# Attention and a depthwise convolution on one core: the convolution's products on TensorE regrouped, and ScalarE's long work moved within a unit

## The chip, the cores and the metric

The kernel runs on one core of one Trainium2 chip. A core has five engines with an instruction stream each: TensorE (PE in the profile; its weight loads are PEld), VectorE (DVE), ScalarE (ACT), GpSimd (POOL) and SyncE (SP, which here only issues DMAs). They run side by side and wait for each other through semaphores. Matrix products are written to PSUM, everything else lies in SBUF. The metric is the device time of one execution in microseconds, as the median of a few runs; lower is better.

## The reference

The input x has 16 images of 384 channels of 32 x 32, in f32. Two layers follow each other, each with a residual and a group norm without weights:

```python
# layer 0: attention over the 1024 positions, 8 heads of 48
x = x + _L0_conv_ref(_gn(x), w_qkv, w_proj, b_proj)
# layer 1: depthwise convolution, 7 x 7, padding 3
x = x + _L1_conv_ref(_gn(x), weight)
# where _L1_conv_ref first symmetrises the weight:
w_sym = (weight + rot90(weight, 1) + rot90(weight, 2) + rot90(weight, 3)) * 0.25
# and _gn(v) normalises over 32 groups of 12 channels of one image
```

The depthwise convolution has one 7 x 7 kernel per channel and adds nothing over channels.

## The kernel before

One image after the other (b = 0 to 15), three tiles of 128 channels each (k = 0, 1, 2). For each image TensorE makes q and k (qk_step, L446), v (v_step, L472) and then 64 steps of attention: s_step (L517) makes the scores of a step, ScalarE takes their exponential (L525), av_step (L537) multiplies with v. Sixteen steps are a unit, four units an image. Scores run four steps ahead of av_step, and seven at a unit's start. The scores lie in one of three PSUM buffers (pool ps_s), the sums of a unit in two (ps_o). When a unit is done, take copies its sums out on ScalarE (L550) and the next unit's av_step may use them. The projection of image b (L598) is made while image b + 1 starts; its residual and its statistics lead to the group norm of layer 1.

The convolution of image b is done during the attention of image b + 1, by VectorE, tile by tile: ScalarE writes the normalised tile with padding (fold_x, "padded", L692) and three scaled copies of it (fold_first, "rows_e", L703, three instructions), and VectorE folds the taps (fold_ops, L721 to L734). A tile takes VectorE some 40 us.

The order of all instructions is written by the program itself, under a manual schedule: each engine runs its own list strictly as it was emitted. A small planner keeps two clocks, clock for TensorE and vclock for VectorE, and emits VectorE's work up to a given time (catch_up, which takes due work from the list later, and otherwise the next piece of the fold, tap). Long work for ScalarE (the applications of a norm, rows_e, squares) waits in the list applies with a due time and a planned cost; act_slot takes from it what is due and not dearer than a limit. Between the steps of the attention between_steps calls it with the limit 4.3 us.

In the last image there is no attention of a next image to hide the convolution. Three tiles are therefore convolved on TensorE (PE_TILES: tile 2 of image 14, tiles 2 and 1 of image 15); VectorE does tile 0 of image 15 at the same time. The normalised tile goes to DRAM (conv_store, L875) and comes back in shifted copies (conv_load, L882): partition (q, c) of a shifted tile holds channel c of 32 from row q on, for q = 0 to 3. A product (conv_on_pe, L913) has 32 channels times 4 rows as its 128 terms and 32 channels of one row out; seven columns and two groups of four rows are 14 taps, for each half of the picture, with four products in one tap, one for every 32 channels. The matrices are the kernel's weights on diagonals (conv_matrices, L863). A finished tile is copied out by ScalarE and added to the residual by an accumulating DMA on GpSimd's queue (conv_on_pe_end, L926 and L927), the last one by VectorE from PSUM, a half at a time (conv_on_pe_half, L934), and stored.

The tail is laid out by hand. fast_finish ends the projection of image 15, fast_end makes its statistics with small products (groups_on_pe, L334) and starts the norm (x1_chains: conv_begin, conv_store). Pieces of the convolution of (14, 2), called conv_piece, are put in between, so that TensorE has work while VectorE makes means and variances. Then a loop runs the rest of the pieces; loads emits the next shifted copies.

Of the kernel before, what the change touches and what calls it, by code (L numbers as in the profile page):

```python
# [16 lines left out]
P = 128  # L17
# [28 lines left out]
def kernel(  # L46
# [73 lines left out]
    def run(general):  # L120
        tag = "g" if general else "f"
        with ExitStack() as stack:
# [79 lines left out]
            eye = wpool.tile([P, P // 4], F32, name="eye")  # L202
# [10 lines left out]
            wsh = wpool.tile([P, 2, 4, 2, KS], F32, name="wsh")  # L213
# [445 lines left out]

            def conv_begin(st, b, k, engine):  # L660
                name = f"xn1_{b}_{k}"
                if general:
                    xn1s[b, k] = npool.tile([P, N], F32, tag="xn1", name=name)
                elif b == B - 1:
                    xn1s[b, k] = flat(epool.tile([P, 2, HALF], F32, tag="e", name=name))
                else:
                    xn1s[b, k] = tpool.tile([P, N], F32, tag="t", name=name)
                st.apply(xn1s[b, k], x1s[b, k], k, engine)
# [149 lines left out]
            SH, CH = 4, P // 4  # L818
            ROWS = H // 2 + 4
            XROWS = H + 2 * PAD + 1  # L820
            XW = XROWS * W

            def conv_prepare():

                w_d = dconv.tile([C, 2 * SH * KS], F32, tag="w", name="w_d")
                zero = tpool.tile([P, N], F32, tag="t", name="zero")[:, 0 : SH * W]
                nc.gpsimd.memset(zero, 0.0)
                w_rows = w_d.rearrange("(k p) t -> p k t", p=P)
                with nc.allow_non_contiguous_dma(reason="small, once"):
                    nc.gpsimd.dma_start(  # L830
                        w_rows[:, :, 0 : KS * KS], wsym.rearrange("p k i j -> p k (i j)")
                    )
                    nc.gpsimd.dma_start(
                        w_rows[:, :, KS * KS :],
                        zero[:, 0 : NK * KS].rearrange("p (k t) -> p k t", k=NK),
                    )
                    for n, k in enumerate(PE_K):
                        for q in range(2 * SH):
                            nc.gpsimd.dma_start(
                                wsh[CH * (q % SH) : CH * (q % SH + 1), n, :, q // SH, :],  # L840
                                bass.AP(
                                    w_d.tensor,
                                    w_d.offset + (k * P * 2 * SH + q) * KS,
                                    [[2 * SH * KS, CH], [CH * 2 * SH * KS, SH], [1, KS]],
                                ),
                            )
                for bk in PE_TILES:
                    xds[bk] = dconv.tile([P, XW], F32, tag=f"x_{len(xds)}", name=f"xd_{len(xds)}")
                    nc.gpsimd.dma_start(xds[bk][:, 0 : PAD * W], zero[:, 0 : PAD * W])
                    nc.gpsimd.dma_start(xds[bk][:, (PAD + H) * W :], zero)  # L850
                for q in range(SH):
                    src = ident[:, CH * q : CH * (q + 1)]
                    if q == 0:
                        nc.gpsimd.tensor_copy(eye, src)
                    else:
                        nc.gpsimd.tensor_tensor(eye, eye, src, ALU.add)

            def conv_matrices(n, dst):

                nonlocal vclock  # L860
                dst = dst[:, 0 : SH * 2 * KS * CH].rearrange("p (i t c) -> p i t c", i=SH, c=CH)
                for i in range(SH):
                    nc.vector.tensor_tensor(  # L863
                        dst[:, i],
                        eye.unsqueeze(1).to_broadcast([P, 2 * KS, CH]),
                        wsh[:, n, i].rearrange("p b d -> p (b d)").unsqueeze(2).to_broadcast(
                            [P, 2 * KS, CH]
                        ),
                        ALU.mult,
                    )  # L870
                mats[PE_K[n]] = dst
                vclock += 2.2

            def conv_store(b, k):
                nc.sync.dma_start(xds[b, k][:, PAD * W : (PAD + H) * W], xn1s[b, k])  # L875

            def conv_load(b, k, h, a):

                t = qkpool.tile([P, 2, N], F32, tag="qk", name=f"sh_{b}_{k}_{h}_{a}")
                xd = xds[b, k]  # L880
                for q in range(SH):
                    (nc.scalar if late.get("tail") and q % 2 else nc.sync).dma_start(  # L882
                        t[CH * q : CH * (q + 1), :, 0 : ROWS * W],
                        bass.AP(
                            xd.tensor,
                            xd.offset + 2 * a * CH * XW + (h * H // 2 + q) * W,
                            [[XW, CH], [CH * XW, 2], [1, ROWS * W]],
                        ),
                    )
                shs[b, k, h, a] = t  # L890


            PE_TAPS = [(d0, dx) for d0 in range(2) for dx in range(-PAD, PAD + 1)]
            PE_TAPS.sort(key=lambda t: t[1] != 0)

            def conv_on_pe(b, k, h, first, last):
                if (b, k) == PE_TILES[-1]:

                    if (b, k, h) not in pss:
                        pss[b, k, h] = ps_o.tile([P, HALF], F32, tag="acc", name=f"ps_conv_{h}")  # L900
                    dst = pss[b, k, h]
                else:
                    if (b, k) not in pss:
                        pss[b, k] = psum(f"ps_conv_{b}_{k}")
                    dst = pss[b, k][:, h, :]
                taps = PE_TAPS
                for n, (d0, dx) in enumerate(taps):
                    if not first <= n < last:
                        continue
                    _, (ox, ix) = region(0, dx)  # L910
                    for i in range(SH):
                        src = shs[b, k, h, i // 2][:, i % 2, 0 : ROWS * W]
                        nc.tensor.matmul(  # L913
                            dst[CH * i : CH * (i + 1), :].rearrange("p (y x) -> p y x", x=W)[:, :, ox],
                            lhsT=mats[k][:, i, d0 * KS + dx + PAD, :],
                            rhs=src.rearrange("p (y x) -> p y x", x=W)[
                                :, SH * d0 : SH * d0 + H // 2, ix
                            ],
                            start=(n == 0),
                            stop=(n == len(taps) - 1),  # L920
                        )

            def conv_on_pe_end(b, k):

                t = tpool.tile([P, N], F32, tag="t", name=f"conv_{b}_{k}")
                nc.scalar.copy(t, flat(pss.pop((b, k))))  # L926
                nc.gpsimd.dma_start(x1s[b, k], t, accum_op=ALU.add)  # L927
                conv_end(b, k)

            def conv_on_pe_half(b, k, h):  # L930

                c = slice(h * HALF, (h + 1) * HALF)
                dst = x1s[b, k][:, c]
                nc.vector.tensor_tensor(dst, pss.pop((b, k, h)), dst, ALU.add)  # L934
                (nc.scalar, nc.sync)[h].dma_start(
                    out[b, k * P : (k + 1) * P].rearrange("p h w -> p (h w)")[:, c], dst
# [164 lines left out]
            def catch_up(to):  # L1101
# [20 lines left out]
                (bk, h, a)  # L1122
                for bk in PE_TILES
                for h in range(2)
# [78 lines left out]
            def between_steps():  # L1203
                catch_up(clock)
                if clock >= act_free:
                    act_slot(4.3, 2.3)

            def x1_chains(b, st):
                nonlocal vclock
                on_pe = [t for t in PE_TILES if t[0] == b]  # L1210
                for k in range(NK - 1, -1, -1):
                    if (b, k) in on_pe:
# [3 lines left out]
                        cuts = (0, 4, 8, 10, 12) if b == B - 2 else (0, KS)  # L1216
                        cuts = (*cuts, len(PE_TAPS))
                        pe_conv.extend((b, k, 0, *c) for c in zip(cuts, cuts[1:]))
                        pe_conv.extend(((b, k, 1, 0, KS), (b, k, 1, KS, cuts[-1])))
# [119 lines left out]
            def loads(n):  # L1339
                while n and pe_loads and pe_loads[0][0] in xn1s:  # L1340
                    (b, k), h, a = pe_loads.popleft()
                    conv_load(b, k, h, a)
                    n -= 1

            def conv_piece():
                nonlocal clock
                b, k, h, first, last = pe_conv.popleft()
                while (b, k, h, 1) not in shs and pe_loads:
                    loads(1)
                conv_on_pe(b, k, h, first, last)  # L1350
                clock += 6.2 * (last - first) / KS
                if last == len(PE_TAPS):
                    loads(2)
                    if (b, k) == PE_TILES[-1]:
                        after(2.0, 0.7, lambda: conv_on_pe_half(b, k, h))
                    elif h == 1:
                        after(6.0, 1.2, lambda: conv_on_pe_end(b, k))
# [52 lines left out]
            def fast_end(b):  # L1410
                assert not applies
                x1_stats[b].groups_on_pe(late["masks"], tap, conv_piece)
                conv_piece()
                x1_chains(b, x1_stats[b])

# [6 lines left out]
            for b, n0, size in [  # L1422
# [9 lines left out]
                if ending:  # L1432
# [4 lines left out]
                    loads(2)  # L1437
                for n in range(n0, n0 + size):
# [3 lines left out]
                    between_steps()  # L1442
# [12 lines left out]
                if b == B - 1:  # L1455

                    if once("mat_0", r >= 16):
                        mat = flat2(xpool.tile([P, NK, N], F32, tag="x", name="mat_0"))
                        conv_matrices(0, mat)
                        late["w3"] = mat[:, 2 * SH * KS * CH :][:, 0:C]  # L1460
# [22 lines left out]
            clock += 7.0  # L1483
            vclock = clock
            after(4.0, 1.2, check_vector)
            while later or state["done"] < len(order) or active or pe_conv:
                if pe_conv:
                    if pe_conv[0][0] == B - 1 and lims:
                        check_tensor(lims.pop())
                    conv_piece()  # L1490
                else:
# [54 lines left out]
```

## Time and profile before

| | us |
|---|---|
| median of 3 runs | 2886.64 (2883.92 to 2887.82) |
| the profiled execution | 2884.99 |
| its span, first to last instruction | 2883.1 |
| granted TensorE clock, mean | 0.998 |
| qk products, busy | 502.5 |
| score and av products, busy | 1088.2 each |
| exponentials on ScalarE, busy | 1024.3 |
| products of the convolution on TensorE, first to last | 2798.99 to 2876.7 |

In a timeline a line gives start, length, engine, source line, operation, output and inputs with their shape, and how many instructions of one kind were put together; in square brackets stands the time that the engine was idle before, and what ended it. A matrix product in f32 leaves two records, and records of neighbouring products overlap, so that the pace is read from one start to the next and not from the length of a record. "ACTq" and "SPq" are DMA issues, which don't count as busy. A line of the list of waits gives who waited for whom, the time in total, how often, and the longest.

### The profile page before, as it was taken

How to read it: one execution, taken by the hardware profiler on the slowest of the kernel's cores; microseconds unless marked ns; L12 is line 12 of the kernel's file. 1: busy time of each engine (PE TensorE's matmuls, PEld its weight loads, DVE VectorE, ACT ScalarE, POOL GpSimd, SP SyncE). 2: the span in 40 equal slices, each digit the busy share in tenths (PEclk: the TensorE clock that was granted, in tenths of full speed). 3: DMA queues.
4: the chain of work that ended last, by engine and by line, in shares of the span. 5: the costliest groups of instructions: out<-in, count | busy, mean ns of one | idle time of the engine just before them, and what ended most of it. 6: DMA issues, size and time to landing. Idle time of an engine off the chain costs nothing.

```text
span 2883.1 us, 46610 instructions
## 1 busy us (share of the span) xinstructions
PE 2860.5 (99%) x19654; PEld 1345.2 (47%) x19654; DVE 2080.2 (72%) x2247; ACT 1650.4 (57%) x1921; POOL 244.9 (8%) x398
## 2 busy tenths in 40 slices
PE   9999999999999999999999999999999999999999
PEld 5343445445454444545445454454544445454333
DVE  4504949858597695968959597695968958598776
ACT  3637647475664746647375573746647475574731
POOL 3201012010101001010010101001010010100000
PEclk9999999999999999999999999999999999999999
DMA  6521121211212112130211212112130211212225
GB/s 241 185 39 47 42 65 31 50 49 44 63 33 59 46 36 64 34 73 24 50 49 44 63 31 55 52 29 65 32 80 24 47 53 42 65 31 43 71 71 134
DMA packets 75467, 169.98 MB, mean 59 GB/s; under 512 B 31872, under 2 KB 33808, under 8 KB 73712
## 3 DMA queue, kind: packets, MB, share of 16 engines
q0 software_dynamic: 32320, 108.03, 14.4%
q1 hardware_dynamic: 41216, 55.21, 7.3%
q10 hardware_dynamic: 1712, 3.67, 0.5%
q8 instruction: 156, 2.56, 0.4%
q14 instruction: 63, 0.52, 0.1%
HBM read 118.61 MB, written 28.72 MB: 51 GB/s over the span
## 4 chain that ended last, share of the span: by engine, by line
PE 92%; ACT 4%; DVE 2%; issue 1%; DMA 0%; SPq 0%; ACTq 0%; DVEq 0%
PE ps_s L517 28%; PE acc L537 27%; PE ps_qk L446 17%; PE ps_v L472 9%; PE ps_proj L598 8%; ACT rows_e L703 2%; PE ps_conv L913 2%; ACT e L525 2%; PE ps_proj_last L642 1%; DVE x L734 1%; DVE side L721 0%; PE warm L1280 0%; DVE rows_o L727 0%; PE ps_st_x L334 0%; DMA sum<-o 0%
## 5 line engine op out<-in xcount | busy, mean ns | idle before, releaser
L525 ACT ACTIVATE e<-ps_s 128x1024 f32<-128x1024 f32 x1024 | 1024.3, 1029 | 452.2 <-PE ps_s L517 451.7
L517 PE MATMUL ps_s<-qk 48*64 48x512 f32 x8192 | 1088.2, 589 | 13.4 <-ACT e L525 13.4
L537 PE MATMUL acc<-e,v 64*64 64x512 f32 x8192 | 1088.2, 589 | 1.3 <-ACT e L525 0.5
L537 PEld LDWEIGHTS acc<-e,v 64*64 64x64 f32 x8192 | 426.1, 132 | 461.6 <-issue 444.7
L517 PEld LDWEIGHTS ps_s<-qk 48*64 48x64 f32 x8192 | 410.1, 132 | 490.2 <-issue 433.5
L721 DVE TENSOR_TENSOR side<-padded 128x1024 f32<-128x1024 f32 x270 | 328.3, 1216 | 355.6 <-ACT padded L692 355.6
L724 DVE SCALAR_TENSOR_TENSOR rows_e<-side,even,rows_e 128x1024 f32<-128x1024 f32 x405 | 508.3, 1273 | 9.9 <-ACT rows_e L703 8.4
L446 PE MATMUL ps_qk<-x,wqk 128*128 128x512 f32 x1152 | 502.5, 595 | 0.0
L446 PEld LDWEIGHTS ps_qk<-x,wqk 128*128 128x128 f32 x1152 | 218.2, 190 | 277.8 <-issue 270.8
L734 DVE TENSOR_TENSOR x<-x,rows_o 128x992 f32<-128x992 f32 (+3 forms) x271 | 310.7, 1147 | 3.0
L734 DVE TENSOR_TENSOR x<-x,rows_e 128x992 f32<-128x992 f32 (+2 forms) x270 | 310.8, 1151 | 0.0
L453 ACT COPY qk<-ps_qk 128x1024 f32<-128x1024 f32 x96 | 97.2, 1012 | 365.0 <-PE ps_qk L446 365.0
L472 PE MATMUL ps_v<-wv,x 128*128 128x384 f32 x768 | 252.6, 486 | 0.0
L598 PE MATMUL ps_proj<-o,wp 128*128 128x512 f32 x540 | 234.2, 592 | 0.0
L472 PEld LDWEIGHTS ps_v<-wv,x 128*128 128x128 f32 x768 | 145.9, 190 | 108.2 <-issue 14.3
L492 ACT COPY v<-ps_v 64x384 f32<-64x384 f32 x256 | 121.6, 475 | 120.6 <-PE ps_v L472 118.0
L724 DVE SCALAR_TENSOR_TENSOR rows_o<-side,odd,rows_o 128x1024 f32<-128x1024 f32 x135 | 172.8, 1280 | 1.6
L724 DVE SCALAR_TENSOR_TENSOR x<-side,even,x 128x1024 f32<-128x1024 f32 x135 | 172.5, 1278 | 0.0
L598 PEld LDWEIGHTS ps_proj<-o,wp 128*128 128x128 f32 x540 | 102.6, 190 | 126.2 <-issue 118.1
L811 POOL DMA_DIRECT2D out<-x x45 | 25.3, 563 | 1510.3 <-DVE x L734 1392.9
L703 ACT ACTIVATE rows_e<-padded,even 128x1024 f32<-128x1024 f32 x135 | 147.0, 1166 | 0.0
L606 ACT ACTIVATE x<-ps_proj,bp 128x1024 f32<-128x1024 f32 x45 | 50.1, 1114 | 167.5 <-PE ps_proj L598 167.5
(142 smaller groups left out, 1030.3 us busy)
## 6 DMA issues: line engine op xcount, KB each, us to landing
x<-in_x POOLq DMA_DIRECT2D x90, 512.0 KB, 5.5
inv<-inv SPq DMA_DIRECT2D x126, 256.0 KB
out<-x POOLq DMA_DIRECT2D x45, 512.0 KB, 3.0
xs<-in_x POOLq DMA_DIRECT2D x42, 512.0 KB, 6.2
qk<-qk POOLq DMA_DIRECT2D x96, 128.0 KB, 4.1
o<-o SPq DMA_DIRECT2D x180, 32.0 KB
sh<-xd SPq DMA_DIRECT2D x32, 160.0 KB
x<-in_x SPq DMA_DIRECT2D x6, 512.0 KB
```

What stands on the lines that cost most here:

```text
L446: nc.tensor.matmul(ps[:, h, :], lhsT=wqk[:, k, s, t, :], rhs=xns[b][:, k, h * HALF : (h + 1) * HALF], start=(k == 0), stop=(k == NK - 1),)
L453: nc.scalar.copy(halves(qks[u][:, s, :]), ps)
L472: nc.tensor.matmul(ps[:, j, 0:C], lhsT=xns[b][:, k, t * P : (t + 1) * P], rhs=wv[:, k, :], start=(k == 0), stop=(k == NK - 1),)
L492: nc.scalar.copy(dst[:, :, 0 : HEADS // 2 * (D + 1)].rearrange("p k (h d) -> p k h d", d=D + 1)[:, :, :, 0:D], src.rearrange("p k (h d) -> ...
L517: nc.tensor.matmul(ps[64 * c : 64 * c + 64, a, :], lhsT=qk[r, 1, 64 * kb : 64 * kb + 64], rhs=qk[r, 0, h * HALF : (h + 1) * HALF], start=True,
L525: nc.scalar.activation(es[n], ps, AF.Exp, scale=SCALE)
L537: nc.tensor.matmul(accs[a][64 * j : 64 * j + 64, :], lhsT=v[rows, kb, c : c + 64], rhs=e[rows, j, :], start=(kb == 0), stop=(kb == 2 * NT ...
L598: nc.tensor.matmul(ps[:, h, :], lhsT=wp[:, t, o * P : (o + 1) * P], rhs=os_[b, t // 2][:, t % 2, h * HALF : (h + 1) * HALF], start=(t == 0 ...
L703: nc.scalar.activation(grid(rows_e[dy - 1]), padded_view(i), AF.Identity, scale=even[:, k, dy, 0:1],)
L721: vec.tensor_tensor(grid(sides[n]), padded_view(i, j), padded_view(i, -j), op)
L724: vec.scalar_tensor_tensor(dst, src, w, dst, ALU.mult, ALU.add)
L734: vec.tensor_tensor(dst, dst, src[:, lo + dy * W : hi + dy * W], op)
```

## The change

One product now has 16 channels times 8 rows as its terms and 16 channels of two neighbouring rows as its 32 outputs. A half is no longer the upper or lower half of the picture but half of the channels (a = 0, 1), of all 16 pairs of rows; seven taps of four products make it complete. The normalised tile is written to DRAM with even and odd rows apart (by_rows, PLANE), so that a shifted copy is again one piece of 2 KB a channel; a load is eight copies of 16 partitions instead of four of 32 partitions.

The outputs now come in the order (16 channels, row of the pair, 16 channels, ...). They are therefore copied to SBUF (conv_take), put in order by two products with a permutation matrix for each half (conv_perm) and added by VectorE from PSUM (conv_add); the accumulating DMAs go. In between_steps the limit for ScalarE's work is 1.4 instead of 4.3 in the last five steps of a unit. In the tail fast_end itself emits padded, then two loads, then rows_e, then the takes and the permutation of (14, 2). The pieces of (14, 2) are cut anew, and the two loads in first_half are gone.

```diff
             def between_steps(r):
                 catch_up(clock)
                 if clock >= act_free:
-                    act_slot(4.3, 2.3)
+                    act_slot(1.4 if r % (2 * NT) >= 11 else 4.3, 2.3)
...
+            RI, CG = KS + 1, P // (KS + 1)
+            NG = P // CG
+            PLANE = (H // 2 + PAD) * W
...
+            def conv_load(b, k, a):
+
+                t = qkpool.tile([P, 2, N], F32, tag="qk", name=f"sh_{b}_{k}_{a}")
+                t = t.rearrange("p a n -> p (a n)").rearrange("p (g n) -> p g n", n=HALF)
                 xd = xds[b, k]
+                for i in range(RI):
+                    (nc.scalar if late.get("tail") and i % 2 else nc.sync).dma_start(
+                        t[CG * i : CG * (i + 1)],
...
+            PE_TAPS = sorted(range(-PAD, PAD + 1), key=lambda dx: dx != 0)
...
+                for n in range(first, last):
+                    dx = PE_TAPS[n]
                     _, (ox, ix) = region(0, dx)
+                    for i in range(NG // 2):
+                        src = shs[b, k, a][:, i]
                         nc.tensor.matmul(
+                            dst[2 * CG * i : 2 * CG * (i + 1), :].rearrange("p (y x) -> p y x", x=W)[
+                                :, :, ox
                             ],
+                            lhsT=mats[k][:, NG // 2 * a + i, dx + PAD].rearrange("p t c -> p (t c)"),
+                            rhs=src.rearrange("p (y x) -> p y x", x=W)[:, :, ix],
                             start=(n == 0),
+                            stop=(n == KS - 1),
+                        )
...
+            def conv_take(b, k, a):
+                if a == 0 or (b, k) not in shs:
+                    shs[b, k] = epool.tile([P, 2, HALF], F32, tag="e", name=f"rows_{b}_{k}")
+                nc.scalar.copy(shs[b, k][:, a, :], pss.pop((b, k, a)))
+
+            def conv_perm(b, k, a):
+
+                nonlocal clock
+                if (b, k) not in pss:
+                    pss[b, k] = psum(f"ps_rows_{b}_{k}")
+                part = slice(64 * a, 64 * a + 64)
+                for row in range(2):
+                    nc.tensor.matmul(
+                        pss[b, k][part, row, :],
+                        lhsT=perm[:, row],
+                        rhs=shs[b, k][:, a, :],
+                        start=True,
+                        stop=True,
+                    )
+                clock += 2.2
+                if (b, k) == PE_TILES[-1]:
+                    after(0.5, 1.3, lambda: conv_add(b, k, part, (nc.scalar, nc.sync)[a]))
+                elif a == 1:
+                    after(3.5 if b < B - 1 else 0.5, 1.3, lambda: conv_add(b, k, slice(0, P), nc.gpsimd))
+
+            def conv_add(b, k, part, queue):
+                dst = by_rows(x1s[b, k][part])
+                nc.vector.tensor_tensor(dst, grids(pss[b, k][part]), dst, ALU.add)
+                queue.dma_start(
...
-                        cuts = (0, 4, 8, 10, 12) if b == B - 2 else (0, KS)
-                        cuts = (*cuts, len(PE_TAPS))
-                        pe_conv.extend((b, k, 0, *c) for c in zip(cuts, cuts[1:]))
-                        pe_conv.extend(((b, k, 1, 0, KS), (b, k, 1, KS, cuts[-1])))
+                        cuts = ((0, 4, KS), (0, 2, KS)) if b == B - 2 else ((0, KS), (0, 2, KS))
+                        for a in range(2):
+                            pe_conv.extend((b, k, a, *c) for c in zip(cuts[a], cuts[a][1:]))
...
             def fast_end(b):
+                nonlocal clock, vclock
                 assert not applies
-                x1_stats[b].groups_on_pe(late["masks"], tap, conv_piece)
-                conv_piece()
+                x1_stats[b].groups_on_pe(late["masks"], tap, lambda: conv_piece(False))
+                conv_piece(False)
                 x1_chains(b, x1_stats[b])
+                clock = now()
+                vclock = clock + 1.0
+                after(0.0, 1.2, check_vector)
+                heapq.heappop(applies)[-1]()
+                loads(2)
+                clock += 3.0
+                heapq.heappop(applies)[-1]()
+                conv_rows()
+                clock += 4.5
...
                     first_half(b)
-                    loads(2)
```

## The prediction

> **What bounds the kernel now.** First the page's busy times, then TensorE's list of waits:
>
> ```profile
> PE 2860.5 (99%) x19654; PEld 1345.2 (47%) x19654; DVE 2080.2 (72%) x2247; ACT 1650.4 (57%) x1921; POOL 244.9 (8%) x398
> ...
> PE ps_s L517 <- ACT e L525: 13.4, 14, 1.0
> ```
>
> TensorE is the bound nearly everywhere, so a microsecond is won where TensorE waits or where it has less to do at the end. One wait repeats 14 times. The timelines of TensorE and ScalarE at one of the 14, and at a unit's end without it:
>
> ```profile
> 442.07 1.90 PE L517 MATMUL ps_s<-qk 48*64 48x512 f32 x16
> 444.93 1.09 PE L517 MATMUL ps_s<-qk 48*64 48x512 f32 x8 [0.96 <-ACT e L525]
> 445.84 2.85 PE L537 MATMUL acc<-e,v 64*64 64x512 f32 x24
> ...
> 498.30 2.85 PE L517 MATMUL ps_s<-qk 48*64 48x512 f32 x24
> 500.88 2.85 PE L537 MATMUL acc<-e,v 64*64 64x512 f32 x24
> ...
> 440.72 3.25 ACT L703 ACTIVATE rows_e<-padded,even 128x1024 f32<-128x1024 f32 x3
> 443.86 1.02 ACT L525 ACTIVATE e<-ps_s 128x1024 f32<-128x1024 f32 x1
> 444.77 1.08 ACT L550 COPY o<-acc 128x512 f32<-128x512 f32 x2
> ```
>
> The three score steps at a unit's end take 445.84 - 442.07 = 3.77 us where rows_e (3.25 us) stands right ahead of the unit's copies, and 500.88 - 498.30 = 2.58 us where it doesn't: 1.19 us lost. A smaller loss is at the ends of twelve batches:
>
> ```profile
> 344.56 4.55 PE L537 MATMUL acc<-e,v 64*64 64x512 f32 x40
> 349.04 1.12 PE L446 MATMUL ps_qk<-x,wqk 128*128 128x512 f32 x2
> ...
> 518.08 4.86 PE L537 MATMUL acc<-e,v 64*64 64x512 f32 x40
> 522.88 1.55 PE L446 MATMUL ps_qk<-x,wqk 128*128 128x512 f32 x3
> ```
>
> 4.48 us without, 4.80 us with rows_e ahead of the last exponential: 0.32 us. Last the tail, timelines of TensorE, VectorE, ScalarE and SP:
>
> ```profile
> 2816.24 14.84 PE L913 MATMUL ps_conv<-sh,mat 128*32 128x496 f32 x144
> ...
> 2853.71 22.95 PE L913 MATMUL ps_conv<-sh,wqk 128*32 128x512 f32 x224
> ...
> 2824.58 1.23 DVE L721 TENSOR_TENSOR side<-padded 128x1024 f32<-128x1024 f32 x1 [5.01 <-ACT padded L692]
> ...
> 2876.75 0.69 DVE L934 TENSOR_TENSOR x<-ps_conv,x 128x512 f32<-128x512 f32 x1 [9.79 <-PE ps_conv L913]
> ...
> 2821.44 1.79 ACTq L882 DMA_DIRECT2D sh<-xd  x4
> ...
> 2824.58 3.27 ACT L703 ACTIVATE rows_e<-padded,even 128x1024 f32<-128x1024 f32 x3
> 2831.12 13.40 ACTq L882 DMA_DIRECT2D sh<-xd  x8
> ...
> 2877.47 0.36 SPq L935 DMA_DIRECT2D out<-x  x1
> ```
>
> TensorE convolves without a gap from 2816.24 to 2876.7, and the last add and store follow. VectorE's own tile (15,0) runs from 2824.58 to 2866.27, 41.7 us without a gap; it has about ten microseconds to spare.
>
> **What the Trainium skill says.** "TensorE: Matmul & The Clock Gate", HAM clock gate: after an idle window of about 3.4 us the matmul clock halves, and needs as long under load to come back. The trace agrees: after the last matmul (2876.7) this row of the windows view grants 0.75 over six microseconds, that is, half a clock in the last three.
>
> ```profile
> 2877.00:2883.00 6.00, 0.00 (x0) 0.00 (x0) 0.44 (x1) 0.00 (x0) 0.00 (x0) 0.75 0.15 52
> ```
>
> The same page, architectural detail: ScalarE and VectorE are strict FIFO; the 5.01 us above, in which ready tiles wait behind ScalarE's DMA issues, fit that. "TensorEngine Tiling (Array Packing)", tiling modes: 128x32 leaves four independent tiles. The trace agrees: 112 products of a tile in 22.95 us are 0.205 us each, where a full 128x128 product takes 0.86 (10.30 us for 12).
>
> **Change 1, ScalarE's gate.** In the new order of instructions no rows_e or other long work stands in the last five steps of a unit; those before a unit's copies now stand three exponentials behind them (where ScalarE has 2.12 us free), and those at a batch's end stand behind its copies, ahead of the first qk copy, for which ScalarE waited 4.28 us. Removed: 14 x 1.19 + 12 x 0.32 = 20.5 us. Cost: rows_e of tile k=0 is about 4.4 us later and VectorE stands on it (its first use at 442.12 follows at once). That is covered by 4.94 us of VectorE's idle before the recip at 2615.24; without cover it would move the statistics, which have 8 us to spare (bs written at 2650.65, read at 2658.94). Taken at nothing; bounds 0 and 5 us.
>
> **Change 2, half the products.** Taps per half go from 14 to 7, products per tile from 112 to 56: 22.95 becomes 11.5 us. Added are four products of 128x64 per tile (perm), 0.86 each, 3.4 us, or 2.6 where the two column halves overlap. Net 8 us less per tile, 24 us for three. Up to the second averages (2816.24) nothing of it shows: the fillers there are 4, 3, 1 x 2 taps, and VectorE's means (2811.16), not the fillers, set the pace.
>
> After 2816.24 the old order had 18 taps in hand (14.84 us), the new one has 5 (4.1 us), so TensorE runs dry at 2820.3. What comes next is perm of tile (14,2), and this is where the working needs the order and the waits of the new program:
>
> (a) ScalarE: xn and padded, now ahead of the loads: done at 2820.2 instead of 2824.55. By itself that gives VectorE 4.3 us.
> (b) Eight DMA issues on ScalarE, four of each of two loads. Each of the second four waits on the semaphore of one of the first load, so the eighth waits for the first load to land. The old 13.40 us above is the same wait. The first load starts at 2822.2, as before (store, then load). It is eight copies of 16 partitions x 8 KB, 1.05 MB. The old pair of loads, 32 partitions a copy, ran at 203 to 233 GB/s (windows 2822 to 2828); that rate gives 4.7 us. Half the partitions may mean half the rate: 9.5 us. I take 6.5, between the two: the six qk copies of 16 partitions (L462, 128 KB each) take 7.5 us in the trace's packets (2494.7 to 2502.3), 104 GB/s, but on one queue, and here are two. Landed 2828.7, last issue (0.45) 2829.2.
> (c) rows_e 3.27: 2832.5. Two takes of 0.53: 2833.5, the first at 2833.0.
> (d) perm after 12 us of idle, so at half the clock: 3 x 1.72 = 5.2 us (bounds 2.6 warm, 6.9 cold without overlap): 2838.2.
> (e) VectorE: its next instruction in order is the add of (14,2), ahead of the fold of (15,0), though it has nothing to do with it. The nearest row is the add from PSUM L934, 0.69 for 512; 1.2 for 1024. The fold starts at 2839.4, not 2824.58.
> (f) the fold, 41.7, and three more adds inside it at 1.2 each (old: two of 0.69, outside): 2884.7.
> (g) the last store to the span's end: 2883.1 - 2877.44 = 5.7. End 2890.4.
>
> So the tail is 7.3 us longer although TensorE works 24 us less: TensorE, with 23 us of convolution and 6.9 of perm left after (d), is done by about 2870 and its halves are ready before VectorE asks for them. The bound moved to VectorE, and VectorE waits on ScalarE, which waits on a DMA.
>
> **Small parts at nothing:** sixteen instead of eight matrix products on VectorE (4.45 us before, about 1 more), hidden by its 4.28 us of idle before the divide at 2750.06. Eight instead of four issues on SP ahead of the inverse of unit 61 (four more, 1.8 us, and 0.4 MB more before it in the ring): the divide is 1 to 5 us later; 0.73 + 3.08 us of VectorE's idle, and 3.02 more before the reciprocal at 2794.81, hide it. Left over at worst 1 us. xn in another order of rows: 0 to 0.4 us on the store, within (b)'s bounds. More memsets and DMAs on GpSimd in batch 2: it is 8% busy. The accumulating DMAs of (14,2) and (15,2) go; nothing waited for them at the end.
>
> **Sum.** 7.3 - 20.5 = -13.2 us: span 2869.9. The profiled run took 2884.99 with a span of 2883.1, so 2871.8 against its own time; the median of the three runs is 2886.64, and -13.2 from it is 2873.4. I forecast 2873.
>
> **Rivals.**
> - Clean tail (0.07): VectorE's fold starts when padded is there, at the old 2824.6. Then 41.7 + 4 x 1.2 + 5.7 end at 2876.8, minus 20.5 is 2856.3, time about 2860. For it: TensorE's work really halves. Against it: the program order on VectorE.
> - The stall moves (0.10): rows_e is not removed from ScalarE, and half or more of the 20.5 us comes back as waits of TensorE further on, or VectorE's 4.4 us of lag is not covered. Ends near 2880 to 2887. Against it: rows_e stands in just that new place once an image already (474.89, three exponentials behind the copies at 471.22), and the products go on at 0.86 us apiece there (475.94, 476.80, 477.66).
> - Slower, by slow loads (0.05): the copies of 16 partitions become the bound. Four loads follow each other from 2822.2; behind the last come 5.7 of taps, 0.5 copy, 1.7 perm, 1.2 add and 5.7: 2837 + 4x. At 58 GB/s x is 18 us, the end 2909 - 20.5 = 2888.5, time 2892; it decides from there. For it: 16 partitions a copy; against: the 104 GB/s above.
> - The gate wins nothing at all (0.04), the tail still costs 7.3: 2894.
>
> **Numbers.** My forecast has 0.74. Its bounds: load 4.7 and perm 2.6 with everything else as taken give 2869.0; load 9.5, perm 6.9 and 2 us less won in the attention give 2880. Toward the clean tail I go down to 2866: range 2866 to 2880, which leaves out most of that rival and of the last three. A measurement of this kernel can tell about 0.2%, 5.8 us, from no change. Faster: 0.73 of the forecast, 0.07, and 0.03 of the moved stall: 0.83. Same 0.085, slower 0.085.
>
> **What would show it.** Right: no wait of ps_s on e of 14 times; TensorE idle for some 12 us after 2800 (in new time), then perm at half clock; VectorE's first fold behind the add of (14,2); the chain's end on VectorE, not on ps_conv. Wrong: a load that lands in 3 us or 15, TensorE's last product after VectorE's last add, or new waits of TensorE inside units.

## The result, and the profile after

| | us | ratio to before, 95% interval |
|---|---|---|
| before, median of 5 runs | 2886.64 (2883.92 to 2887.82) | |
| after, median of 5 runs | 2871.87 (2867.82 to 2874.66) | 0.9948, 0.9934 to 0.9963 |
| span of the profiled execution, before | 2883.1 | |
| span of the profiled execution, after | 2870.9 | |

The change makes the kernel faster by 0.5%. The two profiled spans differ by 12.2 us; the sum of the prediction was 13.2. The five runs of the changed kernel alone spread over 6.8 us. First the page of the changed kernel, its busy times (engine, us, share of the span, number of instructions):

```profile
PE 2832.4 (99%) x19342; PEld 1115.2 (39%) x19342; DVE 2083.9 (73%) x2257; ACT 1649.1 (57%) x1925; POOL 250.6 (9%) x410
```

TensorE is busy for 28 us less, and the span is shorter by less than half of that. TensorE's list of waits (who, for whom, us in total, times, the longest) tells where the rest is:

```profile
PE ps_rows L965 <- ACT rows L956: 15.9, 3, 14.5
...
PE ps_st_x L335 <- DVE mn_x L344: 0.8, 1, 0.8
PE acc L538 <- ACT o L551: 0.6, 1, 0.6
```

The line with 14 waits of ps_s on e is gone. A new one is at the top: one wait of 14.5 us for the copy of rows, that is, for conv_take. The other two are small. The end of the unit that the prediction showed, now in the timelines of the changed kernel (TensorE, ScalarE, VectorE; start, length, operation, how many):

```profile
442.38 2.75 PE L518 MATMUL ps_s<-qk 48*64 48x512 f32 x24
444.96 2.75 PE L538 MATMUL acc<-e,v 64*64 64x512 f32 x24
...
442.75 1.07 ACT L551 COPY o<-acc 128x512 f32<-128x512 f32 x2
443.69 2.93 ACT L526 ACTIVATE e<-ps_s 128x1024 f32<-128x1024 f32 x3
446.51 3.25 ACT L715 ACTIVATE rows_e<-padded,even 128x1024 f32<-128x1024 f32 x3
...
447.70 1.28 DVE L736 SCALAR_TENSOR_TENSOR rows_e<-side,even,rows_e 128x1024 f32<-128x1024 f32 x1 [5.18 <-ACT rows_e L715]
```

The three score steps take 444.96 - 442.38 = 2.58 us instead of 3.77. ScalarE's copies come right after the exponential, three more exponentials follow, and only then rows_e. The price is in the last line: VectorE stands for 5.18 us on rows_e, and catches up later.

Now the tail, in the chain of waits that ended last (start, length, what). It is the part from the applied norm to VectorE's first fold instruction; from there the chain stays on VectorE to the end.

```profile
2798.11 2.83 DMA xd<-xn
2801.12 0.37 ACTq L910
...
2802.47 7.83 DMA sh<-xd
2810.33 0.31 ACTq L910
2810.69 3.23 ACT rows_e L715 x3
2813.92 0.48 ACT rows L956
...
2814.53 4.08 PE ps_rows L965 x8
2818.63 1.23 DVE x L980
2819.86 1.13 DVE side L733
```

This reads as a sentence: the normalised tile is stored, ScalarE issues the loads and waits for the first one to land (7.83 us, then its last issue at 2810.33), only then does rows_e, then the take; TensorE permutes; VectorE adds (14,2); and at 2819.8 the fold begins, though padded, all that its first six instructions need, had been there since 2799.7. TensorE's last product ends at 2851.2, VectorE's last fold instruction at 2865.2.

How long the tail is can be compared best from the instruction that finishes the last norm's scale on VectorE (sc_x, L356 before, L357 after) to the span's end, since the attention ahead of it varies by some microseconds from execution to execution:

| kernel | sc_x at | span | tail |
|---|---|---|---|
| before | 2817.53 | 2883.1 | 65.6 |
| after | 2797.07 | 2870.9 | 73.8 |

20.5 us were won before this point, and 8.2 lost behind it. In what follows "tail" is this stretch, from sc_x to the span's end.

### The profile page after: what moved, and what is told of

The parts are those of the page before. It is cut to its first block, busy times and chain, and to the rows that moved or that the text cites. A ratio compares the mean times of both kernels' runs of the same rounds, so it can differ in the third digit from the quotient of the medians.

```text
span 2870.9 us, 46047 instructions
## 1 busy us (share of the span) xinstructions
PE 2832.4 (99%) x19342; PEld 1115.2 (39%) x19342; DVE 2083.9 (73%) x2257; ACT 1649.1 (57%) x1925; POOL 250.6 (9%) x410
## 4 chain that ended last, share of the span: by engine, by line
PE 95%; DVE 3%; DMA 1%; issue 1%; ACT 0%; ACTq 0%; POOL 0%; SPq 0%; DVEq 0%; POOLq 0%
PE ps_s L518 30%; PE acc L538 30%; PE ps_qk L447 17%; PE ps_v L473 9%; PE ps_proj L599 8%; DVE x L746 1%; DVE rows_e L736 1%; DMA sh<-xd 1%; PE warm L1325 0%; DVE side L733 0%; DMA inv<-rec 0%; DMA inv<-inv 0%; DVE rows_o L736 0%; DVE x L736 0%; DVE x L980 0%
## 5 line engine op out<-in xcount | busy, mean ns | idle before, releaser
L538 PE MATMUL acc<-e,v 64*64 64x512 f32 x8192 | 1040.5, 588 | 0.6 <-ACT o L551 0.6
L518 PE MATMUL ps_s<-qk 48*64 48x512 f32 x8192 | 1040.8, 589 | 0.0
L538 PEld LDWEIGHTS acc<-e,v 64*64 64x64 f32 x8192 | 308.8, 132 | 575.8 <-issue 574.2
L518 PEld LDWEIGHTS ps_s<-qk 48*64 48x64 f32 x8192 | 307.5, 132 | 577.4 <-issue 525.8
```

The lines of the kernel that those rows point to most:

```text
L518: nc.tensor.matmul(ps[64 * c : 64 * c + 64, a, :], lhsT=qk[r, 1, 64 * kb : 64 * kb + 64], rhs=qk[r, 0, h * HALF : (h + 1) * HALF], start=True,
L538: nc.tensor.matmul(accs[a][64 * j : 64 * j + 64, :], lhsT=v[rows, kb, c : c + 64], rhs=e[rows, j, :], start=(kb == 0), stop=(kb == 2 * NT ...
```

## The experiments

Each kernel was timed against the kernel before in the same session, in five rounds, and its ratio is to those runs; lines and tails are of one profiled execution of each.

**The gate taken out of the changed kernel (e1_gate_off).**

```diff
-                    act_slot(1.4 if r % (2 * NT) >= 11 else 4.3, 2.3)
+                    act_slot(4.3, 2.3)
```

> The changed kernel with the limit for ScalarE's long work at 4.3 us in all steps, as before the change; the tail is the changed one. My theory (the gate wins 20.5 us by taking away the waits of TensorE at the ends of units and batches, the halved products win nothing): the 14 waits of ps_s on e come back, time 2871.9 + 20.5 = 2892, slower than the kernel before by some 5 to 7 us. Rival (the gain comes from the halved products, the gate only moves waits): about 2872, within 4 us of the changed kernel.

Measured: 2894.82 us (2893.59 to 2898.53), 1.0035 of the kernel before (1.0021 to 1.0049). Its list of waits of TensorE:

```profile
PE ps_s L518 <- ACT e L526: 14.7, 15, 1.2
```

The stalls are back, and the halved products alone make the kernel slower: 9.1 us above 2885.72, the median of the runs of before beside it. The tail is that of the changed kernel, 73.5 us. In the medians it is 23 us slower than the changed kernel instead of 20.5; in its profile products of the last norm's second averages ran at half the clock, which cost 2.6 us and is taken up below.

**The gate alone, in the kernel before (e2_gate_alone).**

```diff
-                    act_slot(4.3, 2.3)
+                    act_slot(1.4 if r % (2 * NT) >= 11 else 4.3, 2.3)
```

> The kernel before with one line of the change, the lower limit in the last five steps of a unit; convolution and tail are the old ones. My theory: 2886.6 - 20.5 = 2866, some 6 us faster than the whole change, because the old tail was 7 us shorter. Rival (the gain comes from the halved products): about 2886, no difference from before. Between them (gate 13, products 2, say): about 2873.

Measured: 2864.83 us (2860.82 to 2869.34), 0.9932 (0.9918 to 0.9945). That is 20.9 us less than before, and 7.0 less than the whole change, though their intervals still touch (0.9918 to 0.9945 against 0.9934 to 0.9963). The profile is sharper: sc_x comes at 2797.36, 20.2 us earlier than before; the tail is 65.5 us, as before. The two runs together settle the shares: the gate is worth all of the gain and more, the regrouped convolution costs 7 to 9 us in the medians, 8 in the profiled tails.

**The add of (14,2) put behind the first part of the fold (e3_fold_first).** The fold of (15,0) is marked as ready when padded is emitted, and the add is due later:

```diff
-                    after(3.5 if b < B - 1 else 0.5, 1.3, lambda: conv_add(b, k, slice(0, P), nc.gpsimd))
+                    after(16.0 if b < B - 1 else 0.5, 1.3, lambda: conv_add(b, k, slice(0, P), nc.gpsimd))
...
                 heapq.heappop(applies)[-1]()
+                ready_x[len(order) - 1] = clock
                 loads(2)
```

> The changed kernel, with VectorE's add of tile (14,2) put behind the first 20 instructions of the fold of (15,0) instead of ahead of them; ScalarE's and TensorE's order stay. My theory (the tail is set by the order on VectorE: the fold stands behind an add that waits for TensorE): the fold starts when padded is there, about 2799.8 in place of 2819.8, does the six instructions that need padded alone and then waits for rows_e until about 2812; span 2856 to 2857, time about 2858, 14 us faster than the whole change. Rival (the tail is set by TensorE's halved clock and the loads of 16 partitions, so that the add's place doesn't matter): about 2872, and the end of the chain goes over to TensorE or stays.

Measured: 2863.58 us (2863.11 to 2865.67), 0.9926 (0.9912 to 0.9939); tail 63.2 us, 10.6 less than in the changed kernel, where 14 to 15 were expected. VectorE's timeline shows the rest (in brackets the idle time and what ended it):

```profile
2801.75 1.23 DVE L733 TENSOR_TENSOR side<-padded 128x1024 f32<-128x1024 f32 x1 [0.57 <-ACT padded L704]
...
2814.06 1.28 DVE L736 SCALAR_TENSOR_TENSOR rows_e<-side,even,rows_e 128x1024 f32<-128x1024 f32 x1 [5.23 <-ACT rows_e L715]
...
2826.31 0.15 DVE L1378 TENSOR_REDUCE good<-ps_again 1x1 f32<-1x2 f32 x1 [2.65 <-PE ps_again L1376]
```

The fold starts as padded comes and waits for rows_e, as expected. But the instruction good (it reads ps_again, a product of TensorE that checks the sums) had kept its due time and stood now in the middle of the fold, ahead of TensorE: 2.65 us more. So the order on VectorE sets the tail, and not only the add has that power. Of the 5.8 us between the span of 2862.3 and the 2856.5 expected, these are 2.65, and another 2.05 are those by which sc_x comes later than in the changed kernel.

**rows_e ahead of the second load (e4_rows_first).**

```diff
                 heapq.heappop(applies)[-1]()
-                loads(2)
+                loads(1)
                 clock += 3.0
                 heapq.heappop(applies)[-1]()
                 conv_rows()
+                loads(1)
                 clock += 4.5
```

> The changed kernel with the second of the two loads emitted behind rows_e and the takes instead of ahead of them; VectorE's order stays. My theory (ScalarE's DMA issues of the second load hold up rows_e, takes, the permutation and so VectorE's add and fold): rows_e starts about 2802.6 instead of 2810.7, the permutation 8 us earlier and possibly less slowed, the fold at about 2811 to 2812, span 2862 to 2863.5, time about 2864. Rival (the wait for the first load, not the place of the issues, sets it, or the later second load holds up TensorE at the end): 2870 to 2875.

Measured: 2869.51 us (2866.49 to 2871.68), 0.9944 (0.993 to 0.9958): in the time nearly nothing. ScalarE's timeline:

```profile
2807.40 1.80 ACTq L910 DMA_DIRECT2D sh<-xd  x4
2809.24 3.23 ACT L715 ACTIVATE rows_e<-padded,even 128x1024 f32<-128x1024 f32 x3 [3.29 <-issue]
```

From sc_x (2803.36 here) to rows_e it is 5.9 us, where in the changed kernel it is 2810.69 - 2797.07 = 13.6: the four issues of the first load take 1.80 us, and rows_e no longer waits for its landing. The add of (14,2) starts at 2817.19, 13.8 us after sc_x instead of 21.6, and the tail is 66.4 us, 7.4 less: in the tail just what was expected. In the profiled execution the span hides it because sc_x itself came 6.3 us later than in the changed kernel. 2.0 of these lie between the first averages (mn_x) and sc_x, where the same products took longer:

```profile
2799.00 3.15 PE L335 MATMUL ps_st_x<-d_x,wv 128*128 128x1 f32 x14
```

In the changed kernel's profile this group took 1.72 us. The other 4.3 lie far ahead of it, where the instructions are those of the changed kernel: at 156 us TensorE waits 2.41 us (0.63 in the changed kernel), and the 18 records behind the wait take 4.53 us (2.36 there). Both places are taken up below. So the rival, the wait for the load or a late second load, is refuted by the tail and not by the time.

**All loads from SP (e6_sp_loads).**

```diff
-                    (nc.scalar if late.get("tail") and i % 2 else nc.sync).dma_start(
+                    nc.sync.dma_start(
```

> The changed kernel with every load issued by SP, so that ScalarE issues none and waits for none; VectorE's order stays that of the changed kernel. My theory (fold behind the add, the add behind ScalarE's stay in the DMA issues): rows_e directly behind padded (about 2799.7 instead of 2810.7), takes to 2804, the permutation at the full clock because TensorE has been idle for only 4 us, the fold from about 2807 on; span 2859 to 2860, time about 2861, unless one queue for all loads (at the 104 GB/s of the qk copies in the trace of before 4.2 MB take 40 us) keeps TensorE to the end: then the last add is late and the span 2860 to 2864. Rival (slow loads set the tail): one queue instead of two makes it longer than the changed kernel, 2875 or more.

Measured: 2865.30 us (2863.98 to 2869.24), 0.9931 (0.9918 to 0.9945); span 2863.4, tail 67.6 us. TensorE's and VectorE's timelines:

```profile
2802.27 3.90 PE L965 MATMUL ps_rows<-rows,perm 128*64 128x512 f32 x8 [3.49 <-ACT rows L956]
...
2817.48 0.15 DVE L1378 TENSOR_REDUCE good<-ps_again 1x1 f32<-1x2 f32 x1 [4.25 <-PE ps_again L1376]
```

ScalarE does rows_e at 2798.43, directly behind padded, and the fold starts at 2807.35, as expected. Two parts of the expectation fell. The permutation fell to half the clock although TensorE had been idle for only 3.49 us, and good again stopped the fold, for 4.25 us, since the earlier a fold starts, the longer it stands there. Without that wait the span would, by this estimate (2863.4 - 4.25), have been the expected 2859. The four loads took no longer through one queue: in the trace's packets the last landed at 2832.1, 32.3 us after the first issue, against 33.0 (2807.3 to 2840.3) with two queues in e7_fold_rows_check below. "DMA: Bandwidth & Descriptors" of the Trainium skill says so under "Issuing engines are not separate DMA queues": DMAs of several engines run on the same 16 DMA engines and interleave, and issuing from more than one saves only issue time. The rival, 2875 or more, is out.

**Fold first, rows_e first, and good later (e7_fold_rows_check).** The edits of e3_fold_first and e4_rows_first, and:

```diff
+                def verdict():
+                    nc.vector.tensor_reduce(good, ps[0:1, 0, 0:2], AX.X, ALU.add)
+                    nc.vector.tensor_scalar(again, good, -1.0, 2.0 * P, ALU.mult, ALU.add)
+
+                after(10.0, 0.5, verdict)
```

> e3_fold_first and e4_rows_first together, and VectorE's two instructions on ps_again put 10 us later, since in e3 they made VectorE wait 2.65 us for TensorE in the middle of the fold. My theory: the three add up until TensorE is the later engine: VectorE alone would fold from 2799.8 to 2846.5 and the span be 2852; TensorE's last product (2845.8, worked out from e4) gives 1.2 + 2.4 + 5.7 more: span 2852 to 2855, time about 2856, 30 us faster than before. Rival (tail set by clock and loads): no better than e3, 2863.

Measured: 2859.73 us (2856.32 to 2864.85), 0.9910 (0.9896 to 0.9923); tail 58.9 us, 14.9 less than in the changed kernel; expected were 55 to 58. VectorE still waits once:

```profile
2842.12 1.22 DVE L980 TENSOR_TENSOR x<-ps_rows,x 128x1024 f32<-128x1024 f32 x1 [3.87 <-PE ps_rows L965]
```

This is the add of (15,2), which waits for TensorE's permutation: TensorE is now the later engine. Its last product ends 49.2 us after sc_x; it had begun with the first load only at 2817.08, 9.7 us after that was issued.

**The same with all loads from SP (e8_fold_sp_check)** (the edit of e6_sp_loads on top).

> As e7_fold_rows_check, but with all loads issued by SP and none by ScalarE. If two queues load no faster than one (16 partitions a copy set the rate): as e7 or 1 to 3 us better, because ScalarE's takes no longer stand behind DMA issues; span 2851 to 2854. If the number of queues sets the rate: TensorE waits for the third and fourth load, span 2858 to 2864.

Measured: 2860.26 us (2857.68 to 2861.56), 0.9908 (0.9893 to 0.9923); tail 59.4 us, TensorE's last product 49.3 us after sc_x. No difference from two queues: the first of the expected cases, without the 1 to 3 us of gain in it.

**The other adds later (e9_adds_later).**

```diff
-                    after(0.5, 1.3, lambda: conv_add(b, k, part, (nc.scalar, nc.sync)[a]))
+                    after((4.5, 6.0)[a], 1.3, lambda: conv_add(b, k, part, (nc.scalar, nc.sync)[a]))
...
-                    after(16.0 if b < B - 1 else 0.5, 1.3, lambda: conv_add(b, k, slice(0, P), nc.gpsimd))
+                    after(16.0 if b < B - 1 else 5.0, 1.3, lambda: conv_add(b, k, slice(0, P), nc.gpsimd))
```

> e7_fold_rows_check with VectorE's adds of (15,2) and of both halves of (15,1) put later, the last one behind the fold's last instruction. In e7 from the scale of the last norm (sc_x) to the span's end went 58.9 us, of which VectorE waited 3.87 for the add of (15,2). If TensorE is the later engine now (its last product ended 49.2 us after sc_x in e7), only the three fold instructions behind the last add go off the end: 58.9 - 2.4 = 56.5 us. If VectorE's waits for adds were the whole of it: 58.9 - 3.9 - 0.2 = 54.8 us. In times 2855 to 2858.

Measured: 2861.19 us (2856.79 to 2862.00), 0.9918 (0.9905 to 0.9932); tail 61.7 us, longer than in the kernel it was to improve. VectorE's timeline:

```profile
2842.54 1.22 DVE L980 TENSOR_TENSOR x<-ps_rows,x 64x1024 f32<-64x1024 f32 x1 [6.23 <-PE ps_rows L965]
```

The wait went from one add to another. TensorE's last product still ends 49.3 us after sc_x, but the add of the first half of (15,1), whose rows were there at 2835.6, began at 2842.54, as the second half's permutation ended (2842.50).

**TensorE kept busy while it waits (e10_busy).** On top of the last kernel:

```diff
+            def busy(n):
+                ps = psum("ps_busy")
+                t = late["masks"].rearrange("p b c -> p (b c)")
+                for i in range(n):
+                    nc.tensor.matmul(
+                        ps[:, i % 2, 0:256], lhsT=t[:, 0:P], rhs=t[:, 0:256], start=True, stop=True
+                    )
...
+                busy(13)
                 conv_rows()
                 loads(1)
+                busy(4)
```

> e9_adds_later with 17 products added that nobody reads, 128x128x256 on the masks, 13 ahead of the first permutation and 4 behind it, in the time in which TensorE waits for ScalarE and for the first load. They tell what the halved clock costs in the tail. If it matters: the permutation takes 1.9 instead of 3.2 to 4.0 us and the first 28 taps' products (56 records) 5.8 instead of 7.9; TensorE's last product ends 2 to 3 us earlier than in e9 (46 to 47 us after sc_x), and VectorE is the later engine with about 55.3 us from sc_x to the end. If the load and not the clock sets the start and pace of these products: no difference from e9, or up to 1 us longer.

Measured: 2862.85 us (2858.22 to 2863.01), 0.9919 (0.9905 to 0.9932). TensorE's timeline:

```profile
2808.04 2.32 PE L965 MATMUL ps_rows<-rows,perm 128*64 128x512 f32 x8 [0.96 <-ACT rows L956]
...
2812.21 5.90 PE L941 MATMUL ps_conv<-sh,mat 128*32 128x512 f32 x56
...
2820.44 3.48 PE L941 MATMUL ps_conv<-sh,mat 128*32 128x512 f32 x16 [2.31 <-issue]
```

At first the clock does what was hoped: the permutation takes 2.32 us and the first products of the next tile 5.90, where the kernel with the later adds took 4.07 and 6.02. But TensorE then stands for 2.31 us (the profile names no releaser; the products behind are the first that need the second load), and the 16 records behind that run at half the clock again, 3.48 us instead of 1.85. Its last product ends 50.5 us after sc_x instead of 49.3, and the tail is 62.9 us. So a faster clock ahead of that wait doesn't bring TensorE's end forward. Loads and clock are not separated by this run, and what holds TensorE's end at 49.3 us in the other kernels shows only in the next one.

**The two halves of (15,1) in PSUM tiles of their own (e11_halves_apart).** On top of the kernel with the later adds, without the extra products:

```diff
-                if (b, k) not in pss:
-                    pss[b, k] = psum(f"ps_rows_{b}_{k}")
+                if (b, k) not in pss or (b, k) == PE_TILES[-1]:
+                    pss[b, k] = psum(f"ps_rows_{b}_{k}_{a}")
+                rows = pss[b, k]
...
-                        pss[b, k][part, row, :],
+                        rows[part, row, :],
...
-            def conv_add(b, k, part, queue):
+            def conv_add(b, k, part, queue, rows):
                 dst = by_rows(x1s[b, k][part])
-                nc.vector.tensor_tensor(dst, grids(pss[b, k][part]), dst, ALU.add)
+                nc.vector.tensor_tensor(dst, grids(rows[part]), dst, ALU.add)
```

> e9_adds_later with the permuted halves of (15,1) in two PSUM tiles. In e9 the add of the first half stood in VectorE's order behind the emission of the second half's permutation, into the same tile, and waited 6.23 us for that one (61.7 us from sc_x to the end). If it was the shared tile: the wait goes, TensorE's last product (49.3 us after sc_x) ends it with 1.2 for the add and 5.9 for the store, 56.4 us from sc_x to the end, time about 2857. If the add waited for its own half (or for ScalarE, or a buffer): the wait stays and the tail is 61 to 62 us as in e9.

Measured: 2855.69 us (2852.32 to 2855.83), 0.9897 (0.9881 to 0.9914), the fastest median of all, 16 us under the changed kernel and 9 under the gate alone (its interval still touches that of e7_fold_rows_check). The tail is 56.9 us (expected 56.4). Of VectorE's adds only the last waits for TensorE; the other line is TensorE's, the permutation of (15,2):

```profile
2822.04 1.90 PE L966 MATMUL ps_rows<-rows,perm 128*64 128x512 f32 x4 [2.47 <-DVE x L981]
...
2846.19 1.23 DVE L981 TENSOR_TENSOR x<-ps_rows,x 64x1024 f32<-64x1024 f32 x1 [1.64 <-PE ps_rows L966]
```

So it was the shared tile: in this program an add that is emitted behind a second product into its tile waits for that product too, whichever half it reads. Whether the dependence hangs on the tile as such or on the stretch of PSUM that its halves share, the run doesn't tell: the two tiles separate both.

The first line shows what now sets TensorE's end. The permutation of (15,2) waits for VectorE's add of (14,2), by 2.47 us here, 1.88 in e9_adds_later and 1.56 in e8_fold_sp_check, and it starts 25.15 us after sc_x in all three, with the last product ending 49.3 us after it. The scores' three PSUM buffers serve these tiles too, so the likely reason is that the add is what frees the buffer. Putting that add late, which let the fold start, has thus become a limit for TensorE. An add between the old and the new place wasn't tried.

## Why the prediction was right, point by point

**The sum.** 2873 was forecast and 2871.87 measured. Against the profiled spans it was -13.2 and -12.2; the two terms were -20.5 and +7.3, and are -20.5 and +8.2.

**Change 1.** The step was 14 x 1.19 + 12 x 0.32 = 20.5. The last group of products ahead of the tail's idle starts at 2795.79 in place of 2816.24, 20.45 earlier, with all of the 14 waits gone; the gate alone gives 20.2 by sc_x and 20.9 in the medians. The cost of VectorE's lag was taken as nothing, and that holds: VectorE waits 14 times for rows_e, 84.0 us in all, but its waits for the statistics' sums (mv_x, behind a DMA) shrink from 135.4 to 69.7 us and those for the sums of rec from 139.5 to 109.9, and no wait of TensorE's inside the units comes of it. That the stall would move is refuted, and so is that the gate wins nothing.

**Change 2.** In before's coordinates less 20.45, the steps and what came:

| step | predicted | measured |
|---|---|---|
| (a) padded done | 2799.75 | 2799.66 |
| (b) ScalarE's last issue done | 2808.75 | 2810.64 |
| (c) rows_e done | 2812.05 | 2813.92 |
| (d) permutation done | 2817.75 | 2818.6 |
| (e) the fold starts | 2818.95 | 2819.78 |
| (f) the fold ends | 2864.25 | 2865.2 |
| (g) the end | 2869.95 | 2870.9 |

(b) and (d) were mis-sized, in opposite directions. From the first issue of the first load (2801.12) to the landing that frees ScalarE's last issue (2810.3) it took 9.2 us, not 6.5, within the bounds of 4.7 and 9.5. The estimate counted on two queues being faster than one; measured is one rate for both, since one queue was as fast as two (e6_sp_loads, e8_fold_sp_check), and SP went on to issue the second load, which took its share of it. The permutation took 4.1 us instead of 5.2. So the chain of causes was right, but that the totals agree to 1 us is in part luck: 1.9 us too little and 1.0 too much nearly cancel, and the runs of the changed kernel differ by more. The experiments on the order show that (b) and (e) are causes and not only neighbours in time: rows_e ahead of the second load takes 7.4 us off the tail, the fold ahead of the add 10.6, both together with good moved 14.9. The small parts were taken as nothing too. Up to sc_x nothing of them was seen: the whole change brings it 20.5 us forward, the gate alone 20.2.

**The rival of the clean tail** is refuted for this program: it needs the fold to start at padded. e7_fold_rows_check starts it there, and its tail, put behind the changed kernel's sc_x, would end at 2797.07 + 58.9 = 2856.0, near the rival's 2856.3. That they meet is chance: in e7_fold_rows_check the fold starts 2.6 us after sc_x and not 7.1 as in the rival's sum, and VectorE then loses 3.87 us to TensorE. **The rival of the slow loads** needed 18 us a load; it was 9.2 for the first and some 8 each over all four (33.9 us in the changed kernel). Once the order is mended TensorE does wait for a load, 4.8 us in e8_fold_sp_check and 1.1 in the fastest kernel, but its end is set behind that, by the wait for the add of (14,2).

**What the prediction didn't have.** "Up to the second averages nothing of it shows" is true for the profiled execution (mn_x to sc_x 6.5 us before, 6.6 after), but not for all: of the ten profiled kernels with the new convolution (the changed one and nine experiments) five took 8.2 to 9.2 us there, with products that ran at the halved clock, the other five 6.6. The two with the old convolution took 6.5. The new fillers there are shorter, so that TensorE waits 0.8 us for the averages in all ten, and not at all in the two with the old convolution. That this is the cause wasn't tried, and the wait alone doesn't decide it, since five of the ten kept the clock.

## What to carry to other kernels

Halving the work of the engine that bounds a kernel brings nothing in a stage where another engine ends last; look who has the last instruction there, and what stands ahead of its first one in program order. An instruction that only joins a result (an add, a check) belongs in an in-order queue where its input has long been there, but not so late that another engine waits for what it frees, and a tile in PSUM is to be shared only by those that may wait for each other. Where one line of a change can be run alone, run it alone first: here it beat the whole.

## What the runs showed of the hardware

- "TensorE: Matmul & The Clock Gate" of the Trainium skill, HAM clock gate, calls the window of about 3.4 us by which the clock is set free-running; where an idle stretch lies in it should then count, and not its length alone. The runs agree: after 3.49 us of idle in e6_sp_loads the four products of the permutation took 3.90 us, after 3.51 us in e8_fold_sp_check 2.33. After 14.48 us in the changed kernel it was 4.07, and after 0.96 us in e10_busy 2.32. But they don't fit the condition, which the page gives and the prediction took over, that a whole idle window must pass: in e10_busy the clock was halved after 2.31 us of idle (granted 0.50 from 2820.4 to 2822.4), while in e11_halves_apart it was whole after 2.47 us (granted 1.00 from 2822 to 2824). In e4_rows_first it fell at the last norm (granted 1.00 to 2796.7, 0.50 from 2799) behind 0.80 us of idle and a group of one-column products.
- Four products of 128x64 into the two column halves overlap when they follow each other at once: 2.32 us for all four at full clock, where two for one half alone take 1.93.
- The four loads of 16 partitions a copy moved 4.2 MB in 30 to 34 us, 124 to 138 GB/s. Where the DMA engines were busy nearly throughout, the windows of the changed kernel (2805 to 2825) show 126 to 158 GB/s, and with the old loads of 32 partitions (2822 to 2828 before) 203 to 233. The packets changed as well, from 2560 to 2048 bytes; which of the two is the reason was not tried.
- At 150 to 160 us, at the end of a unit of the first image, most of the profiled kernels with the new convolution stand still for up to about 4 us: ScalarE lies idle between the unit's two copies, 1.5 us in the changed kernel and 2.9 in e4_rows_first, and TensorE then waits for the second copy (0.63 and 2.41 us), though all of them but e1_gate_off have the same instructions there. The two kernels with the old convolution show no such wait of TensorE. What it is stays open. Whether it is a part of the 6.8 us by which the five runs of the changed kernel differ is not shown: those of e2_gate_alone, whose profile has no such wait, differ by 8.5.
